# The order of the work in the last eight batches, the slots' order in the first half, and an affine step moved from VectorE to ScalarE, in a fused attention and feed-forward kernel

## The chip, the core and the metric

The kernel runs on one core of one Trainium2 chip. The metric is the device time of one execution in microseconds (us). TensorE is PE in the profile (its weight loads PEld), VectorE is DVE, ScalarE is ACT, GpSimd is POOL; SP is SyncE, which here only issues DMAs. Each engine works through its own instructions in program order, and semaphores tie the engines together.

## What is computed

Sixteen batches of 112 rows of 256 numbers, and for each batch a context of 375 rows of 256, go through four layers, each on a normalized copy (mean and variance of a row) and each added to the rows:

```python
x = x + L0_xattn(layernorm(x), ctx, Wq, Wk, Wv, Wo, bo)   # 16 heads of 64
x = x + L0_ffn(layernorm(x), ...)      # one of two experts by row, plus a shared expert
x = x + L1_xattn(layernorm(x), ctx, ctx, mask)            # one head, no weights
x = x + L1_ffn(layernorm(x), ...)      # int8 weights; one scale from max|layernorm(x)| over ALL rows
```

The second attention is softmax(xn ctxᵀ/16 - (1 - mask) 1e9) ctx. The last layer rounds all normalized rows with one scale, so its products can't start before the last batch's rows are final.

## The kernel before

Everything is float32 except the last product, which is bf16. The first attention is cut into 64 *units* (a batch by a quarter of the heads, `unit`, from L1171), some 10 us each, in which PE is nearly always busy. Other work is hung into the units by hand: `mid(u, f, ...)` puts a call into unit u's middle, `at(u, f, ...)` behind its end (L1019 to L1023). After the units, u goes on counting steps without a unit, up to `LAST`.

The rows are sorted by expert in two halves of seven row tiles; each half is padded to 8 *slots* of 128 rows, which go through one expert each. A slot costs two weight loads of 1024 KB (`slot_weights`, L714; `load_expert`, L697) into two buffers each for the first and the second layer, a load of its rows (`slot_rows`, L722), their transposes (`slot_turn`, L727) and 32 + 16 matmuls (`slot_run`, L812). Slot 0 always has expert 0 and the last slot expert 1; the others' expert is read by SP from `s.index`. Before, the first half's slots run in the order 0 to 7 with the first weights loaded one step ahead; the second half's run from the outside in (0, 7, 1, 6, ...), the first two slots' weights loaded early.

All DMAs that SP issues stand in one queue in program order: the moves of transposed probabilities `pT<-blk` (L490, twelve a unit), the weights, slot rows, contexts (`ctx`, 125 partitions of three 1 KB pieces, L121; `ctxT`, L126 and L130).

The **second attention** of batch b is `second_1` (transposes of the normalized rows, ACT copies them to `xT2`), `second_2` (PE products `pe`; e = pe/16 + mask term; the negated maximum of a row; ACT writes exp(e) over e with its sum), `second_3` (transposes of e) and `second_4` (product with ctx, and DVE adds it to x). For batches 8 to 15 (b >= TAIL) e is written by ACT (L863) and the maximum taken by DVE from the products in PSUM (L872), with a small instruction that scales it (L873). For batches 0 to 7, in units 49 to 56, DVE writes e (L867) and reduces it (L877). ACT and DVE never read the one PSUM tile at the same time; the later in the program waits.

The **tail**: batches 8 to 15 run after all units, one batch a step, in `stages(k)` (L1248), k = u - 82. `do(n, f)` calls f for batch 8 + k - n, and `now(f, list)` calls f for the batches 8 to 15 whose entry in the list is k. What stands ahead of the first `yield` is placed before the step's `extra` calls, the rest behind. In steps -4 to -1 the `extra` calls are the last quarter-runs of the shared expert (`ph_sh`, `hT_sh`, `acc_sh`, L756 on). A batch needs:

- `sort_get` (L828): a gather by POOL of its expert rows, `got`, from DRAM; `sort_add` (L838): POOL adds them to x (L844);
- the l2 statistics, `norm_steps("l2", b)`: DVE `bn_stats` (L271) and `bn_aggr` (L272), POOL variance + eps, power and `nb` (L275, L276, L286); then `rows("l2")`: ACT writes the normalized rows (L300);
- `second_1` to `second_4`, with `second_1` of the next batch between e and the maximum;
- the l3 statistics in the same way, `rows("l3")` on ACT (its `nb` on DVE, but on POOL for batch 15), `third_max` (DVE: max|xn|, L926; POOL adds a bias to x, L929), `third_turn` (L914: PE transposes, ACT copies into `x3T`).

Before, the l2 statistics of batches 12 to 15 stand *ahead* of step 0, 3, 4 and 5, right behind their POOL add, and those of batch 10 ahead of the last quarter-run in step -1. The transposes `third_turn` stand at the end of the step that made the rows.

After step 9, `farthest` (L309) finds max|x - mean| of batch 15 straight from x, so that the scale can be had before its normalized rows; then transposes, maximum, broadcast (`pm`, `top`, `pb`), `xscale`, `rscale`; then `stages(10)` (the normalized rows of batch 15 and their transposes) and eight pairs of batches through `scaled`, `products`, `stored` (L1338 on).

Of the kernel before, what the change touches and what calls it, by code (L numbers as in the profile page):

```python
# [9 lines left out]
F32 = mybir.dt.float32  # L10
# [4 lines left out]
AF = mybir.ActivationFunctionType  # L15
ALU = mybir.AluOpType
AX = mybir.AxisListType
# [3 lines left out]
B, S, D = 16, 112, 256  # L21
SK = 375
# [14 lines left out]
ESCALE = D ** -0.5  # L37
# [17 lines left out]
TAIL = 8  # L55
# [3 lines left out]
def tile_kernel(  # L59
# [26 lines left out]
    nc = tc.nc  # L86
# [3 lines left out]
    const = ctx.enter_context(tc.tile_pool(name="const", bufs=1))  # L90
# [11 lines left out]
    def gen(name):  # L102
        return ps_gen.tile([P, 512], F32, tag="gen", name=name)
# [6 lines left out]
    xs = [xall[:S, xs_place[b], :] for b in range(B)]  # L110
# [92 lines left out]
    negb = const.tile([S, B], F32, tag="negb", name="negb")  # L203
# [36 lines left out]
    def chain(key, steps):  # L240
        chains[key] = {"steps": deque(steps), "from": 0}
# [3 lines left out]
    def late(pool, bufs, more, shape, tag, name):  # L245

        pool, bufs = (fin[0], more) if fin else (pool, bufs)
        return pool.tile(shape, F32, tag=tag, name=name, bufs=bufs)
# [60 lines left out]
    def farthest(mv, y):  # L309

        b = B - 1
        m = mv[:, 0, 0:1]
        d = const.tile([S, 4], F32, tag="far", name="far")
        nc.vector.tensor_reduce(d[:, 0:1], xs[b], AX.X, ALU.max)
        nc.vector.tensor_reduce(d[:, 1:2], xs[b], AX.X, ALU.min)
        nc.vector.tensor_scalar(d[:, 2:3], d[:, 0:1], m, None, ALU.subtract)
        nc.vector.tensor_scalar(d[:, 3:4], d[:, 1:2], m, -1.0, ALU.subtract, ALU.mult)
        nc.vector.tensor_tensor(d[:, 0:1], d[:, 2:3], d[:, 3:4], ALU.max)
        far.append((d[:, 0:1], y))

    far, farthest_of = [], []

    def transposed(dst, src, name):

        pt = gen(f"pt_{name}")
        n = src.shape[0]
        for c in range(DC):
            nc.tensor.transpose(  # L328
                pt[:, c * n : (c + 1) * n], src[:, c * P : (c + 1) * P], ident[:n, :n]
            )  # L330
        nc.scalar.copy(dst, pt[:, : DC * n].rearrange("p (c s) -> p c s", c=DC))  # L331
# [506 lines left out]
    def sort_add(b):  # L838
        t = got.pop(b)
        if b < TAIL:  # L840
            add = lambda: nc.vector.tensor_tensor(xs[b], xs[b], t, ALU.add)
            chain(("l2", b), [add] + norm([b], "l2"))
        else:
            nc.gpsimd.tensor_tensor(xs[b], xs[b], t, ALU.add)  # L844
# [10 lines left out]
    def second_2(b, between=lambda: None):  # L855
        pe = gen(f"pe_{b}")
        for dc in range(DC):
            nc.tensor.matmul(
                pe[:S, :SK], xT2[b][:, dc, :], ctxT2[b][:, dc, :], start=(dc == 0), stop=(dc == DC - 1)
            )  # L860
        e = late(tmp, 1, 2, [S, SK], "e", f"e_{b}")
        if b >= TAIL:
            nc.scalar.activation(  # L863
                e, pe[:S, :SK], AF.Identity, bias=negb[:, b : b + 1], scale=ESCALE
            )
        else:
            nc.vector.tensor_scalar(e, pe[:S, :SK], ESCALE, negb[:, b : b + 1], ALU.mult, ALU.add)  # L867
        between()
        nmax = small.tile([S, 1], F32, tag="nmax2", name=f"nmax2_{b}")
        if b >= TAIL:  # L870

            nc.vector.tensor_reduce(nmax, pe[:S, :SK], AX.X, ALU.max)  # L872
            nc.vector.tensor_scalar(  # L873
                nmax, nmax, -ESCALE, negb[:, b : b + 1], ALU.mult, ALU.subtract
            )
        else:
            nc.vector.tensor_reduce(nmax, e, AX.X, ALU.max, negate=True)  # L877
        den = small.tile([S, 1], F32, tag="den2", name=f"den2_{b}")
        nc.scalar.activation(e, e, AF.Exp, bias=nmax, accum_out=den)
        rdens[b] = den  # L880
        es[b] = e
# [19 lines left out]
    amax = const.tile([S, B], F32, tag="amax", name="amax")  # L901
# [12 lines left out]
    def third_turn(bs):  # L914
        for b in bs:
            if b < TAIL:
                t = tmp.tile([P, DC, S], F32, tag="x3s", name=f"x3s_{b}", bufs=1)
                transposed(t, normed["l3", b], f"x3_{b}")
                nc.scalar.dma_start(out=x3T_d[b], in_=t)
            else:  # L920
                transposed(x3T[0][:, b, :, :], normed["l3", b], f"x3_{b}")

    def third_max(bs):
        for b in bs:
            if b < B - 1:
# [108 lines left out]
    for t in range(NT - 1):  # L1034
        u = done(t) * UN + UN
# [39 lines left out]
    blocks = set()  # L1075
    for c, u in enumerate((16, 24, 32, 47)):
        at(u, shared, c)
        at(u + 2, shared_store, c)
        blocks.add(u)


    s = sorts[0]
    u = NU // 2 + UN
# [2 lines left out]
    at(u + 1, places_parts, s)  # L1086
    at(u + 2, places_shift, s)
    u += 2
    for i in range(s.slots):

        early = i < 2
        mid(u + i - early, slot_weights, s, i, 0)
        at(u + i - early, slot_weights, s, i, 1)
        mid(u + i, slot_rows, s, i)
        mid(u + i + 1, slot_turn, s, i)
        at(u + i + 1, slot_run, s, i)
        blocks.add(u + i + 1)
        mid(u + i + 2, slot_store, s, i)
    u += s.slots + 3
    for b in range(TAIL):  # L1100
        at(u - 2 - (b > 0), sort_get, b)
        at(u - 4, load_xs, b)
        at(u - 2, load_ctxT2, b)
        at(u - 1, load_ctx, b)
        mid(u - 1, sort_add, b)
        mid(u, second_1, b)
        at(u, second_2, b)
        mid(u + 1, second_3, b)
        at(u + 1, second_4, b)
        at(u + 1, third_norm, [b])  # L1110
        mid(u + 3, third, [b])
        u += 1


    s = sorts[1]
    order = [i // 2 if i % 2 == 0 else s.slots - 1 - i // 2 for i in range(s.slots)]
    for j in range(2):
        for part in range(2):
            at(NU - 6 + 2 * j + part, slot_weights, s, order[j], part)
# [18 lines left out]
    for j, i in enumerate(order):  # L1138
        u = FIRST_RUN + j
# [104 lines left out]


    steps = {}

    def stages(k):  # L1248
        def b_of(back):
            b = TAIL + k - back  # L1250
            return b if TAIL <= b < B else None

        def do(back, f):
            b = b_of(back)
            if b is not None:
                f(b)

        def norm_steps(name, b):
            nb_on = nc.gpsimd if name == "l2" or b == B - 1 else nc.vector
            steps[name, b] = norm([b], name, True, nb_on)  # L1260
            for f in steps[name, b][:3]:
                f()

        def now(f, at_k):

            for b, own in zip(range(TAIL, B), at_k):
                if own == k:
                    f(b)

        def rows(name):  # L1270
            return lambda b: steps[name, b][3]()

        no = None
        add_norm = lambda b: (sort_add(b), norm_steps("l2", b))
        now(sort_get, (-4, -4, -3, -3, -2, -1, 0, 0))
        now(sort_add, (-3,))
        now(lambda b: norm_steps("l2", b), (-2,))
        now(rows("l2"), (-1, no, 0, 1, 2, 4, 5, 6))
        now(sort_add, (no, -2))
        now(add_norm, (no, no, -1, no, 0, 3, 4, 5))  # L1280
        yield
        now(lambda b: norm_steps("l2", b), (no, -2))
        now(add_norm, (no, no, no, -1))
        now(rows("l2"), (no, -1))
        if k == -1:
            do(-1, second_1)
        do(0, lambda b: second_2(b, lambda: do(-1, second_1)))
        if k >= 0:
            do(-3, load_ctxT2)
            do(-3, load_ctx)  # L1290
        do(1, second_3)
        do(3, rows("l3"))
        do(2, second_4)
        do(2, lambda b: norm_steps("l3", b))
        do(3, lambda b: third_max([b]))
        do(3, lambda b: third_turn([b]))
        yield

    for u in range(NU + 3, LAST - 1):
# [3 lines left out]
        k = u - STEP_0  # L1303
        part = stages(k)
# [9 lines left out]

    farthest_of[0]()
    d, y = far[0]
    amax1 = const.tile([S, 1], F32, tag="amax1", name="amax1")
    nc.vector.tensor_reduce(amax1, amax[:, : B - 1], AX.X, ALU.max)
    nc.vector.scalar_tensor_tensor(amax1, d, y, amax1, ALU.mult, ALU.max)  # L1319
    pm = gen("pm")  # L1320
    nc.tensor.transpose(pm[:1, :S], amax1, ident[:S, :S])
# [9 lines left out]

    for _ in stages(LAST - 1 - STEP_0):
        pass
    wsx = fin[0].tile([S, D], F32, tag="wsx", name="wsx")
    nc.gpsimd.tensor_scalar(wsx, ws_bc, xscale[:S, :], None, ALU.mult)
    pfs = {}
# [109 lines left out]
```

## Time and profile before

| | us |
|---|---|
| median of 3 runs (983.44 to 983.66) | 983.53 |
| the profiled execution, its own time | 988.04 |
| its span, first to last instruction | 986.3 |
| PE busy in the span | 932.6 (95%) |
| 0 to 893: PE busy | 872.0 of 893 |
| 906 to 964 (tail): PE busy, granted clock | 39.9 of 58, 0.85 |
| 964 to the end: scale, last product, stores | 22.3 |

The profile is of one execution. "Busy" is the sum of instruction times of an engine; the releaser of an idle stretch is the instruction whose semaphore ended it. "PEclk" is the TensorE clock granted, as a share of full speed; in this execution it is 1.00 or 0.50 at a time, and the lower values are means over a stretch.

### The profile page before, as it was taken

How to read it: one execution, taken by the hardware profiler on the slowest of the kernel's cores; microseconds unless marked ns; L12 is line 12 of the kernel's file. 1: busy time of each engine (PE TensorE's matmuls, PEld its weight loads, DVE VectorE, ACT ScalarE, POOL GpSimd, SP SyncE). 2: the span in 40 equal slices, each digit the busy share in tenths (PEclk: the TensorE clock that was granted, in tenths of full speed). 3: DMA queues.
4: the chain of work that ended last, by engine and by line, in shares of the span. 5: the costliest groups of instructions: out<-in, count | busy, mean ns of one | idle time of the engine just before them, and what ended most of it. 6: DMA issues, size and time to landing. Idle time of an engine off the chain costs nothing. (4 is left out here: it accounts for less than half of the span.)

```text
span 986.3 us, 16848 instructions
## 1 busy us (share of the span) xinstructions
PE 932.6 (95%) x5567; PEld 709.4 (72%) x5567; DVE 495.6 (50%) x1277; ACT 466.3 (47%) x1241; POOL 463.3 (47%) x504
## 2 busy tenths in 40 slices
PE   9999999999999999989999999999999999998773
PEld 5677677777777787767787887667776677997452
DVE  5556855455447435643445335675766523222355
ACT  4756565364546545753534434355456521221443
POOL 4756665364445535641322426666465513004434
PEclk9999999999999999999999999999999999999787
DMA  5554543234223323274545523545336411883612
GB/s 183 156 163 95 137 127 75 75 95 97 59 60 80 86 53 81 63 228 109 202 145 204 171 65 82 147 118 139 83 96 189 110 43 55 304 307 110 183 45 75
DMA packets 119910, 120.69 MB, mean 122 GB/s; under 512 B 15806, under 2 KB 107152, under 8 KB 115088
## 3 DMA queue, kind: packets, MB, share of 16 engines
q1 hardware_dynamic: 107664, 97.52, 35.2%
q10 hardware_dynamic: 8144, 11.20, 3.9%
q0 software_dynamic: 4016, 10.90, 3.8%
q8 instruction: 45, 0.74, 0.3%
q14 instruction: 41, 0.34, 0.1%
HBM read 71.19 MB, written 10.62 MB: 83 GB/s over the span
## 5 line engine op out<-in xcount | busy, mean ns | idle before, releaser
L456 POOL TENSOR_SCALAR p<-p,rden 128x375 f32<-128x375 f32 x256 | 314.9, 1242 | 263.9 <-DVE rden L453 256.1
L444 ACT ACTIVATE p<-sc,nmax 128x375 f32<-128x375 f32 x256 | 143.4, 572 | 177.8 <-DVE nmax L435 169.6
L339 PE MATMUL pk<-ctxT,wk 128*128 128x375 f32 x512 | 193.1, 499 | 3.7 <-ACT kT L348 2.3
L360 PE MATMUL pv<-wv,ctxT 128*128 128x256 f32 (+1 forms) x768 | 187.7, 381 | 0.7 <-ACT kT L348 0.7
L360 PEld LDWEIGHTS pv<-wv,ctxT 128*128 128x128 f32 (+1 forms) x768 | 143.8, 188 | 48.7 <-ACT kT L348 1.9
L505 ACT COPY pT<-blk 32x384 f32<-32x384 f32 x256 | 130.0, 508 | 29.5 <-DMA pT<-blk 23.6
L477 DVE STREAM_TRANSPOSE blk<-p 128x384 f32<-128x384 f32 x256 | 132.2, 551 | 8.2 <-POOL p L456 4.7
L339 PEld LDWEIGHTS pk<-ctxT,wk 128*128 128x128 f32 x512 | 90.6, 192 | 55.6 <-issue 9.4
L435 DVE TENSOR_REDUCE nmax<-sc 128x2 f32<-128x750 f32 x128 | 111.8, 911 | 0.6 <-PE sc L427 0.5
L427 PE MATMUL sc<-kT,qT 64*128 64x375 f32 x512 | 98.1, 501 | 0.0
L515 PEld LDWEIGHTS pa<-pT,v 128*64 128x64 f32 (+1 forms) x1536 | 74.4, 136 | 32.6 <-issue 16.1
L373 DVE COPY v<-pv 119x256 f32<-119x256 f32 x64 | 27.0, 423 | 125.2 <-PE pv L360 104.1
L515 PE MATMUL pa<-pT,v 128*64 128x112 f32 (+1 forms) x1536 | 88.3, 263 | 1.5 <-DVE v L373 0.8
L348 ACT COPY kT<-pk 128x375 f32<-128x375 f32 x128 | 61.3, 479 | 48.1 <-PE pk L339 47.7
L427 PEld LDWEIGHTS sc<-kT,qT 64*128 64x128 f32 x512 | 43.9, 186 | 34.1 <-issue 13.5
L748 PE MATMUL acc_sh<-sw,hT_sh 128*128 128x256 f32 x224 | 56.3, 383 | 4.4 <-DVE hT_sh L771 3.6
L275 POOL TENSOR_SCALAR var_l<-mv_l 112x1 f32<-112x1 f32 (+2 forms) x54 | 12.9, 239 | 97.4 <-DVE mv_l L272 88.5
L771 DVE TENSOR_SCALAR hT_sl<-ph_sl,slot_b 128x128 f32<-128x128 f32 x64 | 22.3, 350 | 70.2 <-PE ph_sl L761 70.2
L761 PE MATMUL ph_sh<-ffn_x,sw 128*128 128x256 f32 x224 | 56.3, 382 | 0.5 <-ACT ffn_x L331 0.5
L396 PE MATMUL pq<-xT,wq 128*128 128x224 f32 x256 | 54.2, 354 | 0.0
L773 ACT ACTIVATE hT_sl<-ph_sl,slot_b 128x128 f32<-128x128 f32 x64 | 23.2, 367 | 61.7 <-PE ph_sl L761 50.4
L444 ACT ACTIVATION_READ_ACCUMULATOR p<-sc,nmax 128x1 f32 x256 | 51.9, 203 | 0.0
(222 smaller groups left out, 1195.1 us busy)
## 6 DMA issues: line engine op xcount, KB each, us to landing
pT<-blk SPq DMA_DIRECT2D x732, 48.0 KB
ctxT<-in_ctx_t SPq DMA_DIRECT2D x31, 375.0 KB
ctx<-in_ctx SPq DMA_DIRECT2D x16, 375.0 KB
ew<-in_w ACTq DMA_DIRECT2D x2, 1024.0 KB
x_s<-idle POOLq DMA_DIRECT2D x2, 1024.0 KB, 5.7
sw<-in_sw ACTq DMA_DIRECT2D x2, 1024.0 KB
row<-x_s SPq DMA_DIRECT2D x16, 128.0 KB
y_s<-yrow SPq DMA_DIRECT2D x16, 128.0 KB
```

Of the source, the lines that this page charges most:

```text
L339: nc.tensor.matmul(pk[:, :SK], wk_sb[:, dc, m * P : (m + 1) * P], ctxT[b][:, dc, :], start=(dc == 0), stop=(dc == DC - 1),)
L348: nc.scalar.copy(t, pk[:, :SK])
L360: nc.tensor.matmul(pv[: KP[c], n * UD : (n + 1) * UD], ctxT[b][:, dc, c * P : c * P + KP[c]], wv_sb[:, dc, k * UD : (k + 1) * UD], start=( ...
L427: nc.tensor.matmul(sc[:, j, :SK], qT[g, m][r, i * P : (i + 1) * P], kT[b, m][r, :], start=True, stop=True,)
L435: nc.vector.tensor_reduce(nmax, sc[:, :, :SK], AX.X, ALU.max, negate=True)
L444: nc.scalar.activation(p[:, :SK], sc[:, j, :SK], AF.Exp, bias=nmax[:, j : j + 1], accum_out=den[:, j : j + 1])
L456: nc.gpsimd.tensor_scalar(p, p, rden[:, j : j + 1], None, ALU.mult)
L477: nc.vector.transpose(blocked[u][:, :, h * 32 : (h + 1) * 32], probs[u][h].rearrange("p (n k) -> p n k", k=32),)
L505: nc.scalar.copy(pT[r, :, i, :], of[r, :, i, :])
L515: nc.tensor.matmul(pa[j * DH : (j + 1) * DH, j2 * S : (j2 + 1) * S].rearrange("p (i q) -> p i q", q=QB), vv[b, k][: KP[c], c, h * DH : (h ...
L748: nc.tensor.matmul(self.acc[:n, i, :D], hT[:, i * n : (i + 1) * n], self.wb[:, f, :], start=(f == 0), stop=(f == FC - 1),)
L761: nc.tensor.matmul(ph[:, : self.n], self.wa[:, dc, f * P : (f + 1) * P], self.src[:, dc, :], start=(dc == 0), stop=(dc == DC - 1),)
```

## The change

1. `farthest`: the minimum is written negated, and two small instructions become one `scalar_tensor_tensor`: four DVE instructions in place of five.
2. `second_2`: the path of batches 8 to 15 (ACT writes e, DVE takes the maximum from PSUM and scales it) now holds for all batches.
3. The first half's slots run from the outside in, like the second half's. The weights of the first two (both with an expert known beforehand) are loaded in units 24 to 27, not in 37 and 38.
4. `stages`: the gathers of batches 12 to 15 go to the ends of steps -1 to 2, their adds ahead of steps 1 to 4, and the l2 statistics of batches 10 to 15 to the ends of steps -1 to 4, behind the l3 statistics; the l2 rows are written by ACT behind the l3 rows, a step ahead of their transposes. The add of batch 10 moves to step -2. `third_turn` comes one step later, right behind `second_2`; the context loads go to the step's end. In step 9 batch 14's maximum and the reduction of the maxima stand ahead of batch 15's statistics. `third_turn` of batch 14 falls into `stages(10)`, that of 15 behind it.

```diff
-        d = const.tile([S, 4], F32, tag="far", name="far")
+        d = const.tile([S, 3], F32, tag="far", name="far")
...
-        nc.vector.tensor_reduce(d[:, 1:2], xs[b], AX.X, ALU.min)
+        nc.vector.tensor_reduce(d[:, 1:2], xs[b], AX.X, ALU.min, negate=True)
         nc.vector.tensor_scalar(d[:, 2:3], d[:, 0:1], m, None, ALU.subtract)
-        nc.vector.tensor_scalar(d[:, 3:4], d[:, 1:2], m, -1.0, ALU.subtract, ALU.mult)
-        nc.vector.tensor_tensor(d[:, 0:1], d[:, 2:3], d[:, 3:4], ALU.max)
+        nc.vector.scalar_tensor_tensor(d[:, 0:1], d[:, 1:2], m, d[:, 2:3], ALU.add, ALU.max)
...
-        if b >= TAIL:
-            nc.scalar.activation(e, pe[:S, :SK], AF.Identity, bias=negb[:, b : b + 1], scale=ESCALE)
-        else:
-            nc.vector.tensor_scalar(e, pe[:S, :SK], ESCALE, negb[:, b : b + 1], ALU.mult, ALU.add)
+        nc.scalar.activation(e, pe[:S, :SK], AF.Identity, bias=negb[:, b : b + 1], scale=ESCALE)
...
-    for i in range(s.slots):
-        early = i < 2
-        mid(u + i - early, slot_weights, s, i, 0)
-        at(u + i - early, slot_weights, s, i, 1)
-        mid(u + i, slot_rows, s, i)
...
+    for j, i in enumerate(outer_first(s)):
+        if j < 2:
+            for part in range(2):
+                at(u - 14 + 2 * j + part, slot_weights, s, i, part)
+        else:
+            mid(u + j, slot_weights, s, i, 0)
+            at(u + j, slot_weights, s, i, 1)
+        mid(u + j, slot_rows, s, i)
...
-        now(sort_get, (-4, -4, -3, -3, -2, -1, 0, 0))
-        now(sort_add, (-3,))
-        now(lambda b: norm_steps("l2", b), (-2,))
-        now(rows("l2"), (-1, no, 0, 1, 2, 4, 5, 6))
-        now(sort_add, (no, -2))
-        now(add_norm, (no, no, -1, no, 0, 3, 4, 5))
+        now(sort_get, (-4, -4, -3, -3))
+        now(sort_add, (-3, -3, no, no, 1, 2, 3, 4))
+        now(stats, (-2,))
+        now(rows("l2"), (-1,))
         yield
-        now(lambda b: norm_steps("l2", b), (no, -2))
-        now(add_norm, (no, no, no, -1))
-        now(rows("l2"), (no, -1))
+        now(sort_add, (no, no, -2, -1))
+        now(stats, (no, -2))
         if k == -1:
+            now(rows("l2"), (no, -1))
             do(-1, second_1)
         do(0, lambda b: second_2(b, lambda: do(-1, second_1)))
-        if k >= 0:
-            do(-3, load_ctxT2)
-            do(-3, load_ctx)
+        do(4, lambda b: third_turn([b]))
         do(1, second_3)
         do(3, rows("l3"))
+        now(rows("l2"), (no, no, 0, 1, 2, 3, 4, 5))
         do(2, second_4)
+        if k == B - TAIL + 1:
+            amax1.append(const.tile([S, 1], F32, tag="amax1", name="amax1"))
+            do(3, lambda b: third_max([b]))
+            nc.vector.tensor_reduce(amax1[0], amax[:, : B - 1], AX.X, ALU.max)
         do(2, lambda b: norm_steps("l3", b))
-        do(3, lambda b: third_max([b]))
-        do(3, lambda b: third_turn([b]))
+        now(sort_get, (no, no, no, no, -1, 0, 1, 2))
+        now(stats, (no, no, -1, 0, 1, 2, 3, 4))
+        if k >= 0:
+            do(-3, load_ctxT2)
+            do(-3, load_ctx)
+        if k != B - TAIL + 1:
+            do(3, lambda b: third_max([b]))
         yield
...
     for _ in stages(LAST - 1 - STEP_0):
         pass
+    third_turn([B - 1])
```

More of the change, by code (lines that the diff above doesn't have):

```diff
@@ L861, in second_2 @@
         e = late(tmp, 1, 2, [S, SK], "e", f"e_{b}")
-        if b >= TAIL:
-            nc.scalar.activation(
-                e, pe[:S, :SK], AF.Identity, bias=negb[:, b : b + 1], scale=ESCALE
-            )
-        else:
-            nc.vector.tensor_scalar(e, pe[:S, :SK], ESCALE, negb[:, b : b + 1], ALU.mult, ALU.add)
+        nc.scalar.activation(
+            e, pe[:S, :SK], AF.Identity, bias=negb[:, b : b + 1], scale=ESCALE
+        )
         between()
         nmax = small.tile([S, 1], F32, tag="nmax2", name=f"nmax2_{b}")
[L870 to L877, printed above, removed]
+        nc.vector.tensor_reduce(nmax, pe[:S, :SK], AX.X, ALU.max)
+        nc.vector.tensor_scalar(
+            nmax, nmax, -ESCALE, negb[:, b : b + 1], ALU.mult, ALU.subtract
+        )
         den = small.tile([S, 1], F32, tag="den2", name=f"den2_{b}")
@@ L1079, in tile_kernel, with outer_first @@
         blocks.add(u)
+    def outer_first(s):
+        return [i // 2 if i % 2 == 0 else s.slots - 1 - i // 2 for i in range(s.slots)]
     s = sorts[0]
@@ L1088, in tile_kernel @@
     u += 2
-    for i in range(s.slots):
-        early = i < 2
-        mid(u + i - early, slot_weights, s, i, 0)
-        at(u + i - early, slot_weights, s, i, 1)
-        mid(u + i, slot_rows, s, i)
[L1095 to L1098, printed above, removed]
+    for j, i in enumerate(outer_first(s)):
[6 more added lines that the diff above has]
+        mid(u + j, slot_rows, s, i)
+        mid(u + j + 1, slot_turn, s, i)
+        at(u + j + 1, slot_run, s, i)
+        blocks.add(u + j + 1)
+        mid(u + j + 2, slot_store, s, i)
     u += s.slots + 3
@@ L1115, in tile_kernel @@
     s = sorts[1]
-    order = [i // 2 if i % 2 == 0 else s.slots - 1 - i // 2 for i in range(s.slots)]
+    order = outer_first(s)
     for j in range(2):
@@ L1246, in tile_kernel @@
     steps = {}
+    amax1 = []
     def stages(k):
@@ L1273, in stages @@
         no = None
-        add_norm = lambda b: (sort_add(b), norm_steps("l2", b))
-        now(sort_get, (-4, -4, -3, -3, -2, -1, 0, 0))
-        now(sort_add, (-3,))
-        now(lambda b: norm_steps("l2", b), (-2,))
-        now(rows("l2"), (-1, no, 0, 1, 2, 4, 5, 6))
-        now(sort_add, (no, -2))
-        now(add_norm, (no, no, -1, no, 0, 3, 4, 5))
+        stats = lambda b: norm_steps("l2", b)
+        now(sort_get, (-4, -4, -3, -3))
+        now(sort_add, (-3, -3, no, no, 1, 2, 3, 4))
+        now(stats, (-2,))
+        now(rows("l2"), (-1,))
         yield
-        now(lambda b: norm_steps("l2", b), (no, -2))
-        now(add_norm, (no, no, no, -1))
-        now(rows("l2"), (no, -1))
+        now(sort_add, (no, no, -2, -1))
+        now(stats, (no, -2))
         if k == -1:
+            now(rows("l2"), (no, -1))
             do(-1, second_1)
         do(0, lambda b: second_2(b, lambda: do(-1, second_1)))
+        do(4, lambda b: third_turn([b]))
+        do(1, second_3)
+        do(3, rows("l3"))
+        now(rows("l2"), (no, no, 0, 1, 2, 3, 4, 5))
+        do(2, second_4)
+        if k == B - TAIL + 1:
+            amax1.append(const.tile([S, 1], F32, tag="amax1", name="amax1"))
+            do(3, lambda b: third_max([b]))
+            nc.vector.tensor_reduce(amax1[0], amax[:, : B - 1], AX.X, ALU.max)
+        do(2, lambda b: norm_steps("l3", b))
+        now(sort_get, (no, no, no, no, -1, 0, 1, 2))
+        now(stats, (no, no, -1, 0, 1, 2, 3, 4))
         if k >= 0:
@@ L1290, in stages @@
             do(-3, load_ctx)
[L1291 to L1294, printed above, removed]
-        do(3, lambda b: third_max([b]))
-        do(3, lambda b: third_turn([b]))
+        if k != B - TAIL + 1:
+            do(3, lambda b: third_max([b]))
         yield
@@ L1316, in tile_kernel @@
     d, y = far[0]
-    amax1 = const.tile([S, 1], F32, tag="amax1", name="amax1")
-    nc.vector.tensor_reduce(amax1, amax[:, : B - 1], AX.X, ALU.max)
+    amax1 = amax1[0]
     nc.vector.scalar_tensor_tensor(amax1, d, y, amax1, ALU.mult, ALU.max)
```

## The prediction

> **What bounds the kernel now.** I read the page first, then the table of busy time by stretches, PE's waits, and the timeline where PE waits long. Up to 893 us PE is busy for 872.0 of 893 us, so other engines count there only where PE stands still. From 906 to 964 it is busy for 39.9 of 58 us at a mean clock of 0.85: this tail is bound by waits. These are PE's waits over the whole span (line waited for, total us, times, longest):
>
> ```profile
> PE pt_x L328 <- ACT xn_l L300: 8.8, 5, 3.3
> PE acc_sh L748 <- DVE hT_sh L771: 3.6, 1, 3.6
> PE pt_s L328 <- DMA row<-x_s: 2.9, 1, 2.9
> ```
>
> The first two lie in the tail, the third at 434 us, ahead of the first half's first slot. The timeline shows how the first kind comes about, in step 3 (start, duration):
>
> ```profile
> 929.20 0.72 POOL L844 TENSOR_TENSOR x<-x,got 112x256 f32<-112x256 f32 x1
> 929.96 0.43 DVE L271 BATCH_NORM_STATS2 bn_l<-x 112x6 f32<-112x256 f32 x1 [1.66 <-POOL x L844]
> ...
> 930.52 0.52 DVE L872 TENSOR_REDUCE nmax<-pe 112x1 f32<-112x375 f32 x1
> ...
> 931.38 0.61 ACT L879 ACTIVATE e<-e,nmax 112x375 f32<-112x375 f32 x1 [2.17 <-DVE nmax L873]
> ...
> 932.95 0.64 PE L328 MATMUL pt_x<-ident,xn_l 112*128 112x112 f32 x2 [2.78 <-ACT xn_l L300]
> ...
> 933.38 2.71 PE L858 MATMUL pe<-ctxT,xT 128*112 128x375 f32 x4
> ```
>
> A POOL add for a later batch holds DVE's statistics, these hold the maximum that the current batch needs, the exponents wait for it on ACT, the l3 rows stand behind the exponents, and PE's transposes at the step's end, with all PE work behind them, wait for those rows. Then `pe` takes 2.71 us where undisturbed steps show 1.43. The stretches say why (length, busy us of PE, PEld, DVE, ACT, POOL, granted clock, DMA share, GB/s):
>
> ```profile
> 908.60:912.00 3.40, 0.69 (x3) 0.58 (x4) 0.98 (x3) 0.25 (x1) 2.40 (x5) 0.96 0.11 34
> ...
> 918.90:922.30 3.40, 0.69 (x4) 0.51 (x4) 1.55 (x5) 1.88 (x5) 1.07 (x3) 0.95 0.90 236
> 922.30:925.70 3.40, 3.40 (x10) 2.06 (x11) 0.42 (x3) 2.16 (x6) 0.00 (x0) 0.54 1.07 290
> 929.10:932.50 3.40, 1.07 (x5) 0.54 (x4) 2.33 (x8) 1.23 (x5) 1.88 (x5) 0.96 0.63 197
> 932.50:935.90 3.40, 2.95 (x7) 1.61 (x8) 1.23 (x5) 1.24 (x3) 2.23 (x5) 0.50 0.36 121
> ```
>
> After a stretch in which PE was busy for 0.69 or 1.07 of 3.4 us it runs at half clock for the next one or two. A stall is paid twice.
>
> [...]
>
> **The tail's steps (part 4 of the change).** The starts of e on ACT (L863) are 916.01, 921.36, 925.07, 928.39, 936.13, 940.92, 949.15 and 953.60: steps of 5.35, 3.71, 3.32, 7.74, 4.79, 8.23 and 4.45, together 37.6 us. The three longest are those whose maximum, or whose next one, stood behind an l2 `bn_stats` that waited for a POOL add. The change puts these statistics, of batches 10 to 15, behind all that the step's attention needs of DVE, and the l3 transposes one step after their rows, so neither can hold PE in the step itself.
>
> *Entry.* PE stood for 3.60 us at 907.7 to 911.3: the last `hT_sh` of DVE (910.80) was behind `bn_l` at 910.24, which waited for an add that POOL made at 909.47, behind a gather. With that statistic gone from there, `hT_sh` is bound by its products, done at 904.9. The last `acc_sh` group then follows the one before (906.58, by my count 0.4 earlier, as POOL reaches batch 8's root without a gather in between). Its start goes from 911.31 to about 907.1, it takes 1.03 for 1.68, the transposes 0.36 for 0.58, `pe` 1.43 for 2.18: e of batch 8 comes some 5.5 us earlier (3.6 if only the wait goes and POOL and the clock give nothing).
>
> *Steps.* The four steps that no such wait lengthened have a mean of (3.71 + 3.32 + 4.79 + 4.45)/4 = 4.07. By hand, a new step has on PE: `pe` 1.43, two pairs of transposes 0.36 each, `pp` 0.49, `pa` 1.46, 4.1 us, 3.5 by start to start. On DVE: 0.55 + 0.21 + 0.50 (every other) + 0.20 + 0.15 + 0.48 + twice (0.43 + 0.18) + 0.39, 3.4. On ACT: 0.57 + 0.34 + 0.61 + 0.35 + 0.42 (every other) + two of 0.60, 3.3, and an idle 0.6 before the exponents. On POOL, with a gather (1.0), an add (0.73), two roots (0.8 and 1.1) and a bias add (0.73), 4.4 at most. There are five PSUM tiles a step for four buffers, and `pa` now gets that of `pe`, so it waits for the maximum, 0.57 + 0.55 behind `pe`; with `pa` 1.46 and `pe` 1.43 this loop gives 4.0. I take 4.1 a step, 28.7 for seven: 8.9 us less. Ends: 3.5 (PE alone, 13.1 less) and 4.79 (the longest of the four, 4.1 less).
>
> *Queues passed.* SP's context loads move to the step's end but wait for the same buffers as before. POOL's gathers stand behind the l3 root; from issue to landing they took 2.6 to 7.1 us here, and each has a whole step before its add. PE runs fewer gaps, so it stays at full clock, which the 4.1 contains.
>
> *Last steps.* From e of batch 15 to its x (953.60 to 962.80) PE waited for l3 rows ahead of the warming matmuls; those rows are now a step old at that place: 0.6 less.
>
> *Scale and end.* `far` loses a step of 0.14 (L317), no more: batch 14's maximum and L1318 are moved, but DVE does them after the same x. Against this, the chain at the end grows:
>
> ```profile
> 966.37 0.54 PE pb L1326 x2
> 966.91 0.58 PE pt_x L328 x2
> ...
> 967.75 0.76 ACT x3T L1342
> ```
>
> Now the transposes of batch 14 stand there too, and ACT's copy of them stands *ahead* of batch 15's rows, which ACT wrote at 964.85 beside the scale. So behind `pb` come a copy (0.24 to the next start), the rows (0.60), PE's second transposes (0.58) and only then the copy that released L1342: 1.4 us more, and the last products and stores all follow L1342. Ends 0.8 and 1.6.
>
> Tail: -5.5 - 8.9 - 0.6 - 0.15 + 1.4 = **-13.8 us**.
>
> **First half's slots (part 3).** PE waited 2.94 us at 434.3 for slot 0's rows; the two groups behind took 1.7 us more, from start to start, at half clock. SP issued these rows at 435.00, behind twelve `pT` moves that ran at 0.63 each from 423.39 but stopped from 428.05 to 431.00 until the DMA of slot 0's weights, issued at 421.44 and 422.56, had moved on. Without these loads the moves end at 431.0, the rows land 2.2 later at 433.2, before 434.3. So -2.9 - 1.7 = **-4.6** (-1 if the moves still stop for two thirds of that time). The loads now stand in units 24 to 27, where the shared expert's block in unit 24 gives SP time; a `pT` move is used two units later, and PE waited for one only once in the whole span (0.6). I take nothing for it; a stop of 2.9 in each of four units would have to exceed some ten us before PE saw it.
>
> **ScalarE's e in the first half (part 2).** DVE loses 0.58 (L867) and gains one small instruction (L873: 0.21, but 0.13 to the next start) per batch: 0.45 less, eight times. PE is busy there; what counts is that between 530 and 735 us PE waited 5.8 us in seven stalls for ACT `kT` and DVE `oT`, all behind DVE's queue, which holds L867 right after a wait for POOL (3.67 at 614.8). ACT sat idle before the exponents in seven of eight cases (23.7 and 7.1 us), so its 0.57 is hidden; uncovered it would cost at most 0.57 x 8 = 4.6. Four or five stalls get 0.45 shorter: **-2.0**. If the stalls at 621.8 to 625.2 (PE busy 1.06 of 3.4, then half clock) shrink enough to keep the clock, 1.8 more. Ends -5 and 0.
>
> **Sum.** -13.8 - 4.6 - 2.0 = -20.4. The profiled execution spans 986.3 and took 988.0; its counterpart should span some 966. On the median of 983.53 this gives **963.2**.
>
> **Rivals.**
>
> *The loads set the pace.* From step 0 on SP issues a pair of 375 KB each step, and batch x3T (896 KB) among them; at 918.9 to 925.7 the DMA share is 0.90 and 1.07 at 236 and 290 GB/s, at 928 to 930 only 0.35 at 123 GB/s. A pair takes 2.6 to 6.1 us by these rates. With 6.1, batches 12 to 15 come 6.1 apart: four steps 2.0 longer, -12.4 in all: 971. For it: steps halve in places while bytes stay. Against: contexts are loaded three steps ahead, and PE never waited for one.
>
> [...]
>
> *POOL sets the pace.* Its 4.4 us, with waits for DVE between the two roots, bring steps back to the old mean of 5.37: only entry, slots and part 2 are won, 5.5 + 0.6 + 0.15 - 1.4 + 4.6 + 2.0 = 11.5: 972.
>
> *Slower.* In the tail's seven steps the l2 statistics at the end hold the *next* maximum on DVE, each step waits for a late POOL add, PE falls below a third busy and stays at half clock. Steps of 7.74 and 8.23 show this price. At 8.2 each the steps cost 57.4, 19.8 more, and with the 11.5 won elsewhere the kernel is 8 us slower: 992. It decides from a mean step of 37.6/7 + 11.5/7 = 7.0 us, that is, POOL adds some 3 us late in every step. Only four batches still have an add, and POOL sat idle for up to 7.5 us ahead of a root, which speaks against it.
>
> *Nothing changes:* what the edits free on DVE and PE is hidden elsewhere, or given back behind `pb`: 983. The stalls are PE's own, so I hold little of it.
>
> **Chances.** Forecast 0.66; loads 0.13; POOL 0.09; slower 0.08; nothing 0.04. Loads and POOL are faster too: faster 0.88, same 0.04, slower 0.08, where same is within 0.2%, about what a measurement of this kernel can tell from none. The range: the best ends together (-5.5 - 13.1 - 0.75 + 0.8 - 4.6 - 5) are -28, the worst (-3.6 - 4.1 - 0.75 + 1.6 - 1 - 0) are -8; cutting 1 us at the low end, 956.5 to 976 holds the forecast and both faster rivals.
>
> **What would show it.** Right: no wait of `acc_sh` L748 for `hT_sh`; e of batches 8 to 15 about 4.1 apart, PE at clock 1.00 in most of 906 to 945; no wait of `pt_s` for rows at 434; L1342 starting some 2.2 us behind `pb`'s end, for 0.84 now. Wrong: PE waiting for `ctxT`, POOL's L844 waiting for `got`, DVE's L872 still behind L271, or `pT` waits at 270 to 330 us.

## The result, and the profile after

| | before | after |
|---|---|---|
| median, us (runs) | 983.49 (982.71 to 983.66, 4) | 969.53 (969.46 to 971.86, 4) |
| ratio, 95% interval | | 0.9865 (0.9848 to 0.9882) |
| the profiled execution, its span | 988.04, 986.3 | 969.55, 967.8 |
| PE busy | 932.6 (95%) | 925.3 (96%) |

The change makes the kernel 14.0 us faster; 963.2 was forecast, in a range of 956.5 to 976. The profiled pair differs by 18.5 us, since the profiled execution before was 4.5 us above its own median. PE's longest waits after (line waited for: total us, times, longest):

```profile
PE pe L857 <- DMA ctxT<-in_ctx_t: 4.0, 2, 3.6
...
PE pt_x L327 <- ACT xn_l L300: 2.5, 4, 0.9
```

The waits for normalized rows are down from 8.8 to 2.5 us; those of `acc_sh` for `hT_sh` (3.6) and of `pt_s` for slot rows (2.9) are gone. At the head stands a wait that the tail of the kernel before did not have: the context of batch 12 is late. Batches 12 and 13 in the timeline of after:

```profile
919.63 2.81 PE L857 MATMUL pe<-ctxT,xT 128*112 128x375 f32 x4 [3.58 <-DMA ctxT<-in_ctx_t]
...
925.02 1.49 PE L857 MATMUL pe<-ctxT,xT 128*112 128x375 f32 x4
925.44 0.43 DVE L271 BATCH_NORM_STATS2 bn_l<-x 112x6 f32<-112x256 f32 x1
...
926.00 0.39 DVE L271 BATCH_NORM_STATS2 bn_l<-x 112x6 f32<-112x256 f32 x1
...
927.15 0.55 DVE L867 TENSOR_REDUCE nmax<-pe 112x1 f32<-112x375 f32 x1 [0.24 <-ACT e L861]
...
928.05 0.61 ACT L872 ACTIVATE e<-e,nmax 112x375 f32<-112x375 f32 x1 [0.69 <-DVE nmax L868]
```

Both statistics are done at 926.4, the maximum starts 0.03 us behind e's end (in all 16 batches here, and in the eight of before with ACT's e, by 0.03 or more), and the exponents wait 0.69 us for it, where they waited 2.17 before. That is what the change set out to do. But `pe` of batch 12 waits 3.58 and then takes 2.81. The stretches around it (length, busy us of PE, PEld, DVE, ACT, POOL, granted clock, DMA share, GB/s):

```profile
912.60:916.00 3.40, 3.40 (x17) 2.23 (x15) 2.58 (x10) 1.89 (x6) 1.49 (x3) 1.00 1.11 287
916.00:919.40 3.40, 0.05 (x1) 0.00 (x0) 2.01 (x6) 1.89 (x5) 3.00 (x8) 1.00 0.80 262
919.40:922.80 3.40, 3.17 (x8) 1.86 (x9) 0.00 (x0) 0.32 (x1) 1.63 (x4) 0.51 0.43 133
```

An empty stretch, then one at half clock, and ahead of both a DMA share near 1. The end of the kernel, behind the scale's broadcast `pb`:

```profile
946.48 0.35 PE L1332 MATMUL pb<-top,ones 1*128 1x1 f32 x2
...
947.42 0.34 ACT L330 COPY x3T<-pt_x 128x224 f32<-128x224 f32 x1 [4.25 <-PE pt_x L327]
947.67 0.60 ACT L300 ACTIVATE xn_l<-x,nb_l,y_l 112x256 f32<-112x256 f32 x1
...
948.99 0.34 ACT L330 COPY x3T<-pt_x 128x224 f32<-128x224 f32 x1 [0.72 <-PE pt_x L327]
...
949.23 0.76 ACT L1349 ACTIVATE x3T<-x3T,rounding,rscale 128x448 f32<-128x448 f32 x1
```

ACT's rows of batch 15 stand behind its copy of batch 14, and the first scaled tile on ACT starts 2.40 us behind `pb`'s end, for 0.84 before.

### The profile page after: what moved, and what is told of

Read it like the earlier page. It is cut to its first block, busy times and chain, and to the rows that moved or that the text cites. A ratio compares the mean times of both kernels' runs of the same rounds, so it can differ in the third digit from the quotient of the medians.

```text
span 967.8 us, 16846 instructions
## 1 busy us (share of the span) xinstructions
PE 925.3 (96%) x5567; PEld 705.8 (73%) x5567; DVE 493.2 (51%) x1276; ACT 469.8 (49%) x1249; POOL 462.2 (48%) x504
## 5 line engine op out<-in xcount | busy, mean ns | idle before, releaser
L542 PE MATMUL po<-wo,oT 128*128 128x256 f32 x224 | 51.0, 381 | 0.0
```

## Experiments, first round: which part does what

Each kernel here is the kernel before with some of the change's parts. The kernel before itself, beside them, gave 984.92 (982.9 to 988.55, 17 runs).

**The kernel before once more** (`before_again`, no edit):

> The kernel before, unchanged, for a second profile. The first profiled execution took 988.0 where the timed runs took 983.5, and the changed kernel's took 969.6, just its median. If those 4.5 us lie in the slots' part, the second profile shows units 39 to 40 (first score matmuls) some 18.2 apart, not 22.96, and PE not waiting 2.9 for slot 0's rows. If they lie in the tail, the distance from the last slot's store to the last batch's x is some 63.6, not 68.1. If neither moves, the profile says nothing of the difference.

982.9 us, span 981.2. Its profile is the better partner for comparing traces, and it is used so below.

**Parts 1 and 4 alone** (`tail_only`: the diff's `farthest` and `stages`, not `second_2` and not the slots):

```diff
-        now(sort_add, (-3,))
...
+        now(stats, (no, no, -1, 0, 1, 2, 3, 4))
...
+    third_turn([B - 1])
```

> Parts 1 and 4 alone. If the tail's gain in the profiles (-14.0: -15.1 up to the last batch's x, +1.1 behind) is that of timed runs too, -14 against before, 969.5. If the profiled execution of before was 4.5 slow in its tail, -9.5, 974.

974.37 us (973.34 to 977.93, 6 runs), ratio 0.9896 (0.9873 to 0.9918): 10.2 us less, 8.1 to 12.5 by the interval.

**Part 3 alone** (`slots_only`):

```diff
-    for i in range(s.slots):
+    for j, i in enumerate(outer_first(s)):
```

> Part 3 alone. The profiles say -4.75 from unit 39 to unit 40, which gives 978.7 if nothing behind gives it back; if the wait for slot 0's rows was an event of one profiled execution, 983.5. A new wait in units 24 to 30 would make it slower; the profile of the full change shows none (first scores of units 23 to 39 keep their distance from before to 0.01 us).

979.15 us (977.49 to 979.75, 6 runs), ratio 0.9934 (0.9915 to 0.9953): 4.6 to 8.4 us less. PE's wait for the rows is gone: SP's twelve `pT` moves ahead of them take 8.56 us for 11.49, and it issues them at 432.36 us for 435.00. The distance from unit 39's first score product to unit 40's is 18.44 us. In the four profiles without part 3 it is 22.96, 21.54, 22.78 and 24.27, mean 22.9; in the ten with it, 18.1 to 18.7.

**Part 2 alone** (`e_act_only`):

```diff
-        else:
-            nc.vector.tensor_scalar(e, pe[:S, :SK], ESCALE, negb[:, b : b + 1], ALU.mult, ALU.add)
...
-            nc.vector.tensor_reduce(nmax, e, AX.X, ALU.max, negate=True)
```

> Part 2 alone. By my prediction -2.0, 981.5. By the profile of the full change -0.45 up to unit 57 and +1.7 in unit 57, where ACT's e stands behind copies that wait for DMAs and DVE waits 2.3 for it: +1.2, 984.7, or about nothing if later waits swallow it.

985.71 us (983.79 to 988.62, 12 runs), ratio 1.0007 (0.9992 to 1.0021): nothing. By these ratios the three parts alone add up to some 16 us, and the whole change to 13 or 16 (here and in the second round), so nothing shows that they help or hinder each other. Unit starts show why part 2 brings nothing. Among the profiles that run at half clock in unit 50 (below), those with ACT's e are 0.3 to 0.6 us shorter from unit 49 to 57; from unit 57 to 58 they are 1.7 longer (11.6 for 9.91) wherever ACT writes batch 7's e. Batch 7, in unit 57, after:

```profile
713.07 2.77 ACTq L489 DMA_DIRECT2D pT<-blk  x4
...
715.87 2.07 ACT L504 COPY pT<-blk 32x384 f32<-32x384 f32 x4 [2.57 <-DMA pT<-blk]
...
717.97 0.57 ACT L861 ACTIVATE e<-pe,negb 112x375 f32<-112x375 f32 x1
718.58 0.55 DVE L867 TENSOR_REDUCE nmax<-pe 112x1 f32<-112x375 f32 x1 [2.29 <-ACT e L861]
```

and before:

```profile
719.01 2.07 ACT L505 COPY pT<-blk 32x384 f32<-32x384 f32 x4 [2.55 <-DMA pT<-blk]
...
719.53 0.61 DVE L867 TENSOR_SCALAR e<-pe,negb 112x375 f32<-112x375 f32 x1
...
720.18 0.54 DVE L877 TENSOR_REDUCE nmax<-e 112x1 f32<-112x375 f32 x1
```

From unit 55 on (`LAST_SHORT`), ACT itself issues a third of the `pT` moves: four here, 2.77 us. That is the idle time that the trace puts down to a DMA. Its four copies (2.07 us) stand behind them, and ACT's e behind the copies, though its products were done at 716.3. DVE's maximum stands behind e, and the scores' maximum behind that. Before, DVE wrote e itself while ACT issued and copied.

## Second round: the three losses

Each kernel is the changed kernel with an edit. Beside them the kernel before gave 983.94 (980.18 to 991.0, 11 runs).

**The changed kernel once more** (`after_again`, no edit):

> The changed kernel once more, beside the next three. If its time is its own, 969.5 and 0.4% either way; the kernel before spread over 5.6 us in the last comparison, and if that comes from where the half-clock stretches happen to begin, this one spreads as well, 967 to 973, and in its profile the stall before batch 12 costs between 3.6 (the wait alone) and 5.6 us (with a half-clock stretch behind it).

969.49 us (967.12 to 971.07, 6 runs), ratio 0.9838 (0.9799 to 0.9876), span of the profile 967.1. The wait for `ctxT` is 3.9, and batch 12's step 8.53.

**x3T loaded five steps later** (`x3T_late`):

```diff
     at(
-        STEP_0 + 1,
+        STEP_0 + 6,
         lambda: nc.sync.dma_start(
             out=x3T[0][:, :TAIL, :, :].rearrange("p b c s -> p b (c s)"),
```

> Only the load of x3T (896 KB, on SP's queue) is issued five steps later, when the last contexts have been issued. Theory: SP's issues of 2.3, 3.8, 5.4 and 3.5 us, and with them the late context of batch 12, come from x3T standing ahead of them; then PE's wait for ctxT (4.0 us) is gone, e of batches 11 and 12 are 3.5 to 4.1 apart for 8.2, and 4 to 5 us go: about 965. Rival one, contexts are late by themselves (3000-byte packets on few engines): the wait for ctxT stays above 2 us, and under 2 us are won, 968. Rival two, the step waits for something else as well (POOL's add for the rows of its batch, 2.7 us at 923.9): ctxT's wait goes, but batch 12's stretch stays above 6, 967 to 968. Rival three, x3T then lands too late for the scale: ACT or DVE wait for it behind pb, 971 and more.

965.61 us (964.2 to 968.55, 6 runs), 3.9 below the changed kernel beside it. The long wait for `ctxT` is gone and batch 12's step is 3.96 for 8.53; the next is 5.3 for 4.55. Nothing waits for x3T at the end. Where after had the empty stretch, PE keeps its clock:

```profile
910.20:913.60 3.40, 3.40 (x19) 2.49 (x18) 2.73 (x10) 2.00 (x5) 1.39 (x4) 1.00 0.87 257
913.60:917.00 3.40, 2.56 (x12) 1.29 (x11) 1.92 (x8) 2.63 (x7) 3.00 (x7) 1.00 0.42 139
917.00:920.40 3.40, 2.16 (x12) 1.51 (x11) 2.84 (x10) 2.22 (x6) 2.70 (x6) 1.00 0.62 193
```

The contexts still come only just in time. By the landings recorded in the trace, `pe` of each of batches 12 to 15 starts 0.13 to 0.14 us behind the last landing of its `ctxT`, here, in after and in the three other profiles with x3T late (20 cases of 20); in the two profiles of the kernel before, contexts landed 2.3 to 9.5 us ahead of their `pe`. The step of 5.3 holds such a wait of 1.24 us, which the list of waits puts down to DVE.

That settles which transfer is in the way, not how. SP's own timeline in after looks like a queue that is held by it (start, duration of the issue):

```profile
908.42 0.43 SPq L1238 DMA_DIRECT2D x3T<-x3T_d  x1
908.95 2.34 SPq L130 DMA_DIRECT2D ctxT<-in_ctx_t  x1
...
911.72 3.76 SPq L809 DMA_DIRECT2D x<-x_d  x1
...
916.42 5.38 SPq L130 DMA_DIRECT2D ctxT<-in_ctx_t  x1
```

The context of batch 12 is issued right behind x3T (908.95), and by the trace's DMA records none of the 3000-byte packets of a `ctxT` (128 each) landed from 910 to 915, while x3T's 1024 packets of 896 bytes landed from 910 to 917. The third round takes x3T out of that queue.

**Batch 14's transposes ahead of the last maximum** (`turn14_early`):

```diff
-        do(4, lambda b: third_turn([b]))
+        if k <= B - TAIL + 1:
+            do(4, lambda b: third_turn([b]))
...
         do(2, second_4)
+        if k == B - TAIL + 1:
+            do(3, lambda b: third_turn([b]))
```

> Only the transposes of batch 14 and their copy on ACT go ahead of the last maximum, into the last step. Theory: the end of the changed kernel lost 1.0 us between the last maximum and the first scaled tile because ACT's copy of batch 14 stands ahead of the rows of batch 15; with it out of the way this stretch is 2.5 to 2.9 for 3.73 us, 1.0 us or a little less in all: 968.6, ratio to the changed kernel 0.999. Rival: the copy or the transposes now stand before the last maximum, and far is later by as much (the stretch from x of batch 15 to the maximum above 2.79 or the stretch before it above 7.93): nothing is won.

968.05 us (967.53 to 969.47, 6 runs), 1.4 below the changed kernel, with ranges that overlap; the stretch itself is clear. From the last maximum to the first scaled tile it takes 2.05 us (after 3.73, `after_again` 4.44), and the stretches ahead of the maximum stay at 7.94 and 2.78. Batch 15's rows now start before the scale is known:

```profile
945.87 0.60 ACT L300 ACTIVATE xn_l<-x,nb_l,y_l 112x256 f32<-112x256 f32 x1 [1.73 <-DVE amax L1328]
...
946.69 0.35 PE L1335 MATMUL pb<-top,ones 1*128 1x1 f32 x2
...
947.66 0.76 ACT L1352 ACTIVATE x3T<-x3T,rounding,rscale 128x448 f32<-128x448 f32 x1
```

The first scaled tile starts 0.62 us behind `pb`'s end, for 2.40 in after.

**These two, and batch 7's e on DVE** (`three_edits`):

```diff
-        nc.scalar.activation(
-            e, pe[:S, :SK], AF.Identity, bias=negb[:, b : b + 1], scale=ESCALE
-        )
+        if b == TAIL - 1:
+            nc.vector.tensor_scalar(e, pe[:S, :SK], ESCALE, negb[:, b : b + 1], ALU.mult, ALU.add)
+        else:
+            nc.scalar.activation(
+                e, pe[:S, :SK], AF.Identity, bias=negb[:, b : b + 1], scale=ESCALE
+            )
```

> The changed kernel with three edits: x3T loaded five steps later, batch 14's transposes ahead of the last maximum, and the e of batch 7 alone written by DVE again (unit 57, where ACT's e stands behind copies that wait for pT: 1.7 us). If the three costs are independent: 4.5 + 1.0 + 1.7 = 7.2 us less than the changed kernel, 962 to 963. If the wait of unit 57 is given back a few units later (as units 60 to 63 did with 2.5 us in the changed kernel), 963 to 965. If x3T is not what holds the contexts, 967.

963.96 us (961.18 to 966.93, 6 runs), ratio to before 0.9785 (0.9747 to 0.9824), 5.5 below the changed kernel. Unit 57 to 58 is 9.92 us again, 1.7 less. Whether some of it is given back later can't be told: from unit 58 to 63 it takes 49.17 us, and the changed kernel 48.68 and 49.76 in its two profiles.

## Third round: queue or engines, and the two moves of the tail

The kernel before beside these: 985.01 (983.23 to 987.86, 9 runs).

**x3T at its old step, issued by ACT** (`x3T_on_act`):

```diff
-        lambda: nc.sync.dma_start(
+        lambda: nc.scalar.dma_start(
```

> The changed kernel with the x3T load at its old step, but issued by ACT instead of SP. Theory: what held the context of batch 12 is the order in SP's queue, x3T ahead of it; on another queue SP issues the contexts of batches 11 and 12 without it, PE's wait for ctxT falls below 1.5 us, batch 12's step is about 4 to 5, and the time is that of the kernel with x3T five steps later, 965.6 (within 1.5). Rival: the engines' time is what is short, 896 KB in 1024 packets beside the contexts; then the wait for ctxT stays at 3 to 5 us and the time at 969. A third way: ACT itself is held by the issue, as SP was, for 2 to 5 us; then e or the exponents of batch 9 or 10 come that much later and the time is 969 to 972.

971.02 us (970.92 to 971.37, 4 runs): nothing is won. ACT's issue took 0.38 us and held nobody, and PE waited as before:

```profile
920.28 2.81 PE L857 MATMUL pe<-ctxT,xT 128*112 128x375 f32 x4 [3.83 <-DMA ctxT<-in_ctx_t]
```

**My theory of SP's order falls, and the rival holds, but more narrowly than I put it.** The summary of the DMA queues from 908 to 916 us in this run (packets, MB, share of the 16 engines' time), q1 SP's queue, q10 ACT's, q0 POOL's:

```profile
q1 hardware_dynamic: 674, 1.06, 42.7%
q10 hardware_dynamic: 1040, 0.92, 42.3%
q0 software_dynamic: 96, 0.23, 12.7%
```

Together 97.7%: in this stretch the engines have hardly any time left. They serve both queues: from 913 to 915 us 193 data packets of SP's queue landed and 208 of ACT's. So contexts that no longer stand behind x3T in a queue still share the engines with it.

But PE's wait, from 916.45 to 920.28, lies behind this stretch, and only some parts of the context are late in it. The trace records sixteen landings for a `ctxT` or x3T and five for a `ctx` (besides one update at the end of the issue, ahead of its data). Of batch 12's `ctxT` eleven parts had landed by 916.63, the other five from 919.24 to 920.14, and `pe` starts at 920.28; in after it is 917.45, 918.58 to 919.49, and 919.63. These five come right behind the five of batch 11's `ctx` here (917.60 to 918.36) and behind the last five of x3T in after (917.52 to 917.70). I read this as five engines that carry every `ctx`, and their share of `ctxT` and x3T besides, with little change in the order among these. That is inferred from counts and times, as the trace does not name the engines. (The expectation of `x3T_late` has the 3000-byte packets on few engines; those of a `ctxT` land in sixteen parts, the 1 KB pieces of a `ctx` in five.) By the packets of after from 917 to 935 us (means of 47 ns for 1 KB and 0.14 us for 3000 bytes) one pair of contexts keeps five engines busy for 75 x 0.047 + 8 x 0.14 = 4.6 us, an estimate on that reading; the last three steps of `x3T_late` have a mean of 4.63.

**The transposes back in the step of the rows, the statistics left at its end** (`turn_in_step`):

```diff
-        do(4, lambda b: third_turn([b]))
...
+        do(3, lambda b: third_turn([b]))
         yield
...
-    third_turn([B - 1])
```

> The changed kernel with the transposes of the normalized rows back in the step of the rows, at the step's end, as before the change (the last batch's then again in the drained step); statistics stay at the step's end. It parts the change's two moves in the tail. If the statistics alone freed the maximum: steps and time as in the changed kernel, 968 to 970 (with the 1.0 us at the end won back). If the transposes a step later carry part of the gain: each full step is longer by PE's wait for the rows (0.6 to 3.3 us in the kernel before), at 0.6 for six steps 4 us more, 973; at the 1.8 mean of the kernel before 11 more, 980.

970.1 us (969.12 to 972.5, 5 runs), as the changed kernel. PE's waits for rows rise again, but the longest is half of the 3.3 before:

```profile
PE pt_x L327 <- ACT xn_l L300: 6.4, 7, 1.5
```

The seven steps take 30.73 us (after 29.50, `after_again` 29.69), from e of batch 15 to its x 8.71 (7.93), from the last maximum to the first scaled tile 2.47 (3.73, 4.44). So the statistics bring nearly all of part 4's gain; the transposes' move wins some 2 us in the steps and gives 1.3 to 2.0 back at the end.

**ScalarE's e left out, beside the kernel with three edits** (`edits_dve_e`, `b == TAIL - 1` above replaced by `b < TAIL`; `three_again`, no edit):

> The kernel with three edits, but with e of all eight batches of the first half written by DVE, as before the change; beside the next one it measures what ScalarE's e is worth once batch 7 is left out. From the unit starts of the changed kernel, batches 0 to 6 gained 0.45 us up to unit 57, so 0.5 us more than the next: 964.5 against 964.0. If nothing is left of it: within 0.3. If the half-clock stretch near unit 50, which the three edits did not have, depends on it: 1.7 to 2 us more, 966.

> The kernel with three edits once more, beside the last: 964.0, between 961 and 967 as in its first six runs.

964.7 us for `edits_dve_e` (964.15 to 965.2, 5 runs) and 965.98 for `three_again` (964.4 to 967.15, 5 runs). In the traces batches 0 to 6 do gain 0.36 us from unit 49 to 58, but the times give no sign of it: part 2 is worth nothing that these runs can show, even without its loss. The three variants with x3T late (965.6 with that edit alone, 964.9 for all eleven runs with three edits, 964.7 with DVE's e) are not told apart by these runs; all beat the changed kernel's 969.5 by about 4 to 5 us.

## Why the prediction was right, and where its terms were not

The stretches of the tail in five profiles, from the timelines of DVE and ACT (us): start of the last slot's `yrow`; from there to e of batch 8; the steps of e from batch 8 to 15; e of batch 15 to its x; to the last maximum; to the first scaled tile on ACT; from there to the last add.

| | yrow | to e 8 | steps | sum | to x 15 | to max | to scaled | to end |
|---|---|---|---|---|---|---|---|---|
| before | 893.75 | 22.26 | 5.35 3.71 3.32 7.74 4.79 8.23 4.45 | 37.59 | 8.72 | 2.74 | 2.69 | 11.55 |
| before_again | 891.01 | 23.23 | 4.82 2.91 4.24 7.56 4.46 5.98 4.45 | 34.42 | 8.72 | 2.74 | 2.49 | 11.56 |
| after | 889.27 | 16.01 | 2.59 2.91 3.49 8.21 4.07 4.31 3.92 | 29.50 | 7.93 | 2.79 | 3.73 | 11.55 |
| after_again | 887.31 | 16.33 | 2.59 2.91 3.48 8.53 4.55 3.71 3.92 | 29.69 | 7.95 | 2.77 | 4.44 | 11.55 |
| x3T_late | 887.07 | 16.34 | 2.60 2.90 3.49 3.96 5.30 4.04 4.54 | 26.83 | 7.94 | 2.77 | 4.43 | 11.57 |

The direction, the mechanism of the tail and the slots were right. The tail's -13.8 met -14.0 in the profiled pair, but by errors that cancel, and -10.4 in the second pair.

| term | forecast | profiled pair | second pair |
|---|---|---|---|
| entry | -5.5 | -6.3 | -6.9 |
| seven steps | -8.9 | -8.1 | -4.7 |
| last steps | -0.6 | -0.8 | -0.8 |
| far | -0.15 | 0.0 | 0.0 |
| scale and end | +1.4 | +1.0 | +1.9 |
| slots (unit 39 to 40) | -4.6 | -4.75 | -3.2 |
| e on ScalarE (unit 49 to 58) | -2.0 | +1.3 | +1.4 |

- **Entry: right.** `acc_sh` waits no more for `hT_sh`, the transposes take 0.36 us and `pe` 1.52 (0.58 and 2.18 before); the whole came out 0.8 to 1.4 us larger than forecast.
- **Steps: three sizes were off.** First, 4.1 was taken for every step. The first three (2.59, 2.91, 3.49) are shorter, as the pipeline is still filling: the l3 rows begin in step 3, the transposes in step 4. Second, the one step of 8.2 to 8.5 is the rival of the loads: "PE never waited for one" held only at the old pace. The other full steps came as forecast, 3.7 to 4.55, but partly by luck: the 4.1 was worked out from PE, the other engines and the PSUM buffers, and in after each of them begins right behind the landing of its context. Third, the old steps' 37.6 was one execution's; in the second it was 34.4, and taking the sum on the median of 983.53 counted stalls that the median does not have. By these two executions that alone is 3.2 us.
- **Rivals.** The loads: 971 was given, and the measured 969.5 lies nearer to it than to 963.2. In after the loads do set the pace from batch 12 on, but at 3.9 to 4.3 us a step and not the rival's 6.1 (PE stands idle for at most 0.4 us in these steps, so its own work is nearly as long); only the step with x3T beside them is 8.2. Without that one (`x3T_late`) it is 965.6. POOL's pace did not come: full steps stay below 5.37 but for the one that waits for its context. Its add at 923.89 did wait, 2.68 us for its batch's rows from DRAM, beside the late context. Slower: no maximum stands behind statistics any more.
- **Far and end.** The instruction saved brought nothing: the new order puts batch 14's maximum and the reduction ahead of batch 15's statistics, so DVE's `far` (done at 945.39) and POOL's power (945.35) are both ready 2.6 to 2.7 us behind the start of the last add to x, where they were ready after 2.6 and 2.1. The loss at the end is the one forecast; `turn14_early` takes it back.
- **Slots: right,** in size and in cause; distances of units 24 to 38 changed by 0.01 us at most, so the early loads cost nothing. The slots' new order and the early loads were not tried apart. The second pair's -3.2 is smaller because `before_again` waits as long (3.2 us) but has no half clock behind it: the 1.7 us of that are not in every execution.
- **Part 2: the step that failed.** ACT's 0.57 was called hidden, because ACT sat idle before the exponents in seven of eight cases. The eighth case was the one that counted: in unit 57 ACT is not idle but issues DMAs and copies for 4.8 us, and e stands behind that: 1.7 us. Its queue ahead of the new instruction was not read batch by batch. And 0.45 less on DVE in seven batches hardly reached PE: 0.3 to 0.6 in all, not "four or five stalls" of 0.45.
- **What adds up.** Against the forecast's 963.2 x3T beside the contexts cost 3.9 us (by medians) and part 2 brought 0 for 2.0; these two are 5.9 of the 6.3 us missed. The rest is rough bookkeeping: the too large credit for the old steps is about balanced by the short first ones and the entry.

## What to carry to other kernels

When a stage is made faster, work out anew whether its loads still fit: bytes per step over the new step's time against the highest rate the trace shows, with every other transfer of that stretch. Where a load lands in few parts, as `ctx` does in five, read the landings of the parts beside the mean share: in `x3T_on_act` the share was 97.7% up to 916, and PE waited until 920.28 for five parts of a `ctxT`. A transfer that is needed late belongs behind those needed soon (3.9 us here); another queue did not help here (971.0 us). A `ctx` cut so that it lands in more parts was not tried. Before an instruction is moved to an engine that looks idle, read that engine's queue at each place where it will stand, not on average. And take the old stalls from more than one execution before they are counted as gain.

## What the runs showed of the hardware

**The same stall cost 0 or 1.7 us more, by where it fell on a grid of 3.41 us.** `three_edits` and `three_again` are one kernel. In unit 50 PE stands still twice for 1.1 us in both, with 0.4 us of work between. In the trace's clock records every half-clock stretch of an execution begins on one grid of 3.41 us (the eight in before at 437.30, 625.03, 911.75, 921.99, 932.23 and so on, the five in after at 8.08, 622.48, 919.44, 946.75 and 960.40, within 0.01 us), and in each execution the grid lies elsewhere. Cut by this grid, the stall falls into two windows of `three_edits`:

```profile
614.98:618.39 3.41, 2.32 (x13) 1.91 (x12) 3.28 (x7) 2.03 (x7) 2.68 (x4) 1.00 0.79 193
618.39:621.81 3.42, 2.32 (x9) 1.51 (x10) 2.07 (x7) 2.87 (x10) 2.54 (x3) 1.00 0.97 253
```

and nearly whole into one of `three_again`:

```profile
617.97:621.39 3.42, 1.31 (x5) 0.88 (x6) 3.09 (x10) 3.42 (x12) 2.11 (x4) 1.00 0.90 235
621.39:624.80 3.41, 3.41 (x8) 2.31 (x8) 0.49 (x2) 2.36 (x6) 3.41 (x3) 0.50 0.87 203
```

The first keeps its clock with 2.32 us of work in each window; the second has 1.31 in one and runs at half clock in the next. Unit 51 comes 17.24 and 18.95 us after unit 50. No stretch had to be empty for that: in the fourteen profiles, PE was busy for at most 1.61 us in each of 62 full-clock stretches of the grid that a half-clock one followed, and for more in all but two (1.46 and 1.58) of the 3724 that kept the clock; in before and after alone, for 0.00 to 1.44 us in 13 of the first kind and for at least 1.89 in the 541 of the second. Whether all of the 5.6 to 10.8 us over which the kernel before spreads comes from this stays open: the start (first scores at 11.6 to 14.1 us) and units 60 to 63 (28.4 to 31.0) vary too.

**A long DMA issue on SP ran on while the mean share of the engines was a third.** In the tails of after, `x3T_late` and `x3T_on_act` an issue on SP took 0.3 to 0.7 us or 2.3 to 5.4, with x3T in SP's queue or without. During the longest, 5.38 us from 916.42 in after:

```profile
918.70:921.80 3.10, 2.17 (x4) 1.26 (x5) 0.61 (x3) 0.00 (x0) 2.28 (x5) 0.62 0.33 115
```

This issue and three like it (`x3T_on_act` 917.52, `x3T_late` 912.39 and 917.10) end 0.1 to 0.6 us ahead of the first landing of the `ctx` of two batches before. What holds the issue, these runs do not show.
